# Keys' squares read from the diagonal of their products with one another, in a gated-delta-rule kernel

## The chip, the cores and the metric

The kernel runs on one core of one Trainium2 chip. The metric is the device time of one launch in microseconds, the median of several runs. The engines are called by the names of the profile: PE (TensorE; PEld is its weight load), DVE (VectorE), ACT (ScalarE), POOL (GpSimd) and SP (SyncE, which only issues transfers here).

## The reference

Four sequences of 512 tokens and 512 channels pass through two blocks. The first mixes channels over time (`cond`), projects to queries, keys, values and gates, runs a gated delta rule over chunks in 16 query/key heads and 32 value heads of 128, and projects back; the second mixes again (`cond2`) and applies a binarized linear layer. What the change touches is the norm of the keys and what uses it:

```python
k = _rmsnorm(k) * inv                       # x * rsqrt(mean(x*x, -1) + eps), per token and head
k_beta = k * beta[..., None]
M = where(stril, einsum('bhncd,bhnmd->bhncm', k_beta, k) * decay, 0)
T = solve_triangular(eye + M, eye, lower=True)
v_c = T @ v_beta;  k_cumdecay = T @ (k_beta * exp(g))
...                                         # scan over the chunks with a state of 128 x 128
```

The kernel uses chunks of 128 tokens. It never scales the keys themselves: the reciprocal root `rk` of each token's sum of squares is folded into factors for each token and value head (`br`, `nbr`, `nbe`).

## The kernel before

The work is cut into 64 units, one for each sequence (batch) and query/key head, `n = 16 * batch + head`. One loop step `i` interleaves pieces of five units: `K` (six ahead: the keys of unit i+6 are made and their matrix prepared), `F` (the front of unit i: values, queries, the inverse), `C` (the chunk recurrence of the unit before), `O` and `W` (its output, two and three before). The interleaving is written out by hand in `plan` (L937), a list of 22 slots; each engine executes its own instructions in exactly the order in which the slots issue them. Nothing is reordered by a scheduler.

What is issued in which slot, as far as it matters here (slots counted from 0):

- slots 5 to 7: `project(K, 1)` makes the keys' projection on PE; `tap` and `taps` (L486) apply the 4-tap convolution, the first tap on ACT into a tile `y`, three more on DVE, each adding to `y` from the PSUM tile `ps_p`.
- slot 8: `silu(K, 1)` (L490) on ACT gives the keys `k`, features on partitions. Slot 9: `square(K, 1)` (L496) on ACT.
- slot 11: `norms(K, 1)` (L501) on PE, four products of a square's 128x128 block with a column of ones, so that each token's sum of squares stands on its own partition (`pss`). In the trace each product is two weight loads and two products, eight rows in all.
- slot 12: `key_norm(K)` (L555) on DVE adds the epsilon, and `root_start` (L512) makes a first guess of the reciprocal root with two integer instructions; `key_root(K)` (L562) refines it on POOL and makes the factors `br`, `nbr`, `nbe`. After `key_norm`, in the same slot, DVE has the last scan of the channel mixing, where there is one.
- slot 13: `taps(F, 3)` on DVE. Slot 14: the state update of chunk 2 (`chunk_t_end`, L856) on DVE, silu of slab 3 on ACT.
- slot 16: `chunk_r(C, 3)` and `key_pairs(K)` (L578) on PE: each chunk's keys times themselves, into a PSUM bank `ps_kk`; also the tap of slab 0 and `chunk_r_end` (L804, the tile `r`) on DVE.
- slots 17 and 18: `key_matrix(K)` (L585) on DVE multiplies `ps_kk` by `nbr` and the decay; `chunk_w(C, 3)` (L821) on PE uses `r`.
- slots 19 and 20: `key_blocks` (L597) and `inverse_load` (L648) issue transfers on SP.

Some units also carry a channel-mixing job (`"wkv"` entries; `EXTRA`, L1015): heads 3, 4, 5 and 7 mix the first block's input for the next batch, heads 9, 11, 12 and 13 the second block's. Such a job puts four scans, a long reciprocal and, at slot 18, `wkv_end` (L307) on DVE; for the second block it also stores its result through SP. In batch 0 the units transpose the raw weights, too, which adds work on PE and ACT; later batches load them transposed. Head 8 of the first three batches computes the gates of the next batch.

PSUM banks come in four tags, with 2, 3, 1 and 2 buffers (`banks`, L90). `ps_kk` shares the single `inv` bank with the steps of the triangular inverse (slots 3 to 11) and with the query products (slot 20).

Before the loop the keys of the first six units are made in a start-up of their own (`first_norm`, L1140): their norms are collected in one tile, one root is taken for all, and then `key_pairs` and `key_matrix` follow for each.

## Time and profile before

| what | value |
|---|---|
| median of 3 runs | 3418.11 us (3409.30 to 3420.46) |
| the profiled execution: time, span | 3405.61 us, 3403.5 us |
| mean granted TensorE clock | 0.972 |
| PE busy | 3235.8 us, 95% |
| DVE busy | 2125.1 us, 62% |
| ACT busy | 1854.7 us, 54% |
| POOL busy | 1453.4 us, 43% |
| DMA, mean | 96 GB/s |

The spans of the units follow from the starts of `chunk_w` of chunk 0 on PE: about 46.1 us without channel mixing in batches 1 to 3, 46.9 with the second block's and 48.2 with the first block's, and some 3.5 us more in batch 0. A busy share is an average over all of these. In a timeline each row gives the start, the time from the first to the last instruction of a merged group, the engine, the source line (here always that of the recording helper, so one goes by the tiles), the operation, the tiles as out<-in, the shapes, how many instructions are merged, and in brackets the engine's idle time before it with what ended it. A row for PE that ends after the next one starts is normal: products are pipelined.

### The profile page before, as it was taken

What the parts mean: (1) busy time and instruction counts of PE and PEld (TensorE: products, weight loads), DVE (VectorE), ACT (ScalarE), POOL (GpSimd) and SP (SyncE); (2) the same over time, 40 slices, a digit from 0 to 9 for tenths busy, and PEclk for the clock granted to TensorE, in tenths of its full rate; (3) what the DMA queues carried; (4) which work ended last, traced back from release to release, by engine and by line L of the source; (5) the groups of instructions that cost most, each with busy time, mean ns of one, the idle gap of its engine ahead of it and who ended that gap; (6) DMA issues with size and microseconds to landing.
All of it is one profiled execution on the core that took longest, in us unless ns stands there. A gap on an engine that the chain in (4) does not pass through costs nothing.

```text
span 3403.5 us, 57390 instructions
## 1 busy us (share of the span) xinstructions
PE 3235.8 (95%) x20096; PEld 2232.8 (66%) x20096; DVE 2125.1 (62%) x4443; ACT 1854.7 (54%) x5016; POOL 1453.4 (43%) x3018
## 2 busy tenths in 40 slices
PE   6659999999999999999999999999999999999968
PEld 3336767767767666677766667667777667766634
DVE  7345766667656777667665777767755656667420
ACT  2436666666665655555555655555565556555411
POOL 3315445264533647265533556264624334453011
PEclk8669999999999999999999999999999999999978
DMA  2224434344434323234223332234332233232132
GB/s 69 91 63 113 139 116 125 113 121 139 125 105 134 99 67 96 81 93 120 73 86 103 108 87 87 62 95 119 87 96 80 92 90 99 80 90 71 44 101 78
DMA packets 424704, 326.51 MB, mean 96 GB/s; under 512 B 217377, under 2 KB 332577, under 8 KB 423394
## 3 DMA queue, kind: packets, MB, share of 16 engines
q1 hardware_dynamic: 420194, 320.75, 32.0%
q8 instruction: 161, 2.64, 0.3%
q10 hardware_dynamic: 4224, 2.10, 0.2%
q14 instruction: 125, 1.02, 0.1%
HBM read 251.18 MB, written 71.57 MB: 95 GB/s over the span
## 4 chain that ended last, share of the span: by engine, by line
PE 79%; DVE 8%; ACT 4%; issue 3%; DMA 2%; SPq 0%; POOL 0%; ACTq 0%; POOLq 0%; DVEq 0%
PE ps_p L79 21%; PE ps_out L79 13%; PE ps_z L79 12%; PE ps_w L79 4%; PE ps_s L79 4%; PE ps_j L79 4%; PE ps_i L79 3%; PE ps_o L79 3%; DVE y L79 3%; PE pss L79 3%; PE ps_st L79 2%; PE ps_kq L79 2%; DVE f L79 2%; PE ps_h L79 1%; PE ps_v L79 1%
## 5 line engine op out<-in xcount | busy, mean ns | idle before, releaser
L79 PE MATMUL ps_p<-cT,w 128*128 128x512 f32 x2000 | 948.9, 606 | 13.5 <-ACT w L79 13.5
L79 DVE SCALAR_TENSOR_TENSOR y<-ps_p,cw,y 128x511 f32<-128x511 f32 (+2 forms) x768 | 570.6, 743 | 474.5 <-ACT y L79 460.9
L79 PEld LDWEIGHTS ps_p<-cT,w 128*128 128x128 f32 x2000 | 349.2, 191 | 329.9 <-issue 274.6
L79 PE MATMUL ps_z<-w,cT 128*128 128x256 f32 x2048 | 476.5, 379 | 0.0
L79 PE MATMUL ps_out<-hT,wo 128*128 128x512 f32 x1024 | 463.7, 596 | 0.0
L79 PEld LDWEIGHTS ps_z<-w,cT 128*128 128x128 f32 x2048 | 373.7, 190 | 42.5
L79 PEld LDWEIGHTS ps_out<-hT,wo 128*128 128x128 f32 x1024 | 184.7, 190 | 186.2 <-issue 168.3
L79 DVE TENSOR_TENSOR xT<-xT,ps_out 128x512 f32<-128x512 f32 x256 | 174.8, 683 | 183.7 <-PE ps_out L79 183.3
L79 POOL TENSOR_TENSOR L<-L,t 128x30 f32<-128x30 f32 (+14 forms) x450 | 262.6, 584 | 35.3
L79 POOL TENSOR_TENSOR rs_t_k<-rs_y_k 128x4 f32<-128x4 f32 x174 | 48.3, 277 | 522.5 <-DVE rs_y_k L79 513.4
L79 ACT ACTIVATE qs<-ps_s,eg 128x128 f32<-128x128 f32 x384 | 120.1, 363 | 261.1 <-DVE r L79 259.7
L79 POOL TENSOR_TENSOR dkd<-dkd,far_d 128x1024 f32<-128x1024 f32 x64 | 151.3, 2365 | 255.2 <-DMA dkd<-gsc 210.2
L79 DVE SCALAR_TENSOR_TENSOR o<-o,rs_y_o,nz 128x128 f32<-128x128 f32 x512 | 238.2, 521 | 3.7 <-POOL rs_y_o L79 3.7
L79 POOL TENSOR_TENSOR t<-L 128x30 f32<-128x30 f32 (+14 forms) x450 | 224.7, 499 | 30.3
L79 ACT ACTIVATE dkt<-dkt,gsum 128x128 f32<-128x128 f32 x512 | 162.9, 392 | 130.2 <-POOL dkt L79 130.1
L79 ACT ACTIVATE y<-ps_p,cw 128x512 f32<-128x512 f32 x256 | 175.2, 684 | 75.9 <-PE ps_p L79 65.6
L79 ACT ACTIVATE wd<-ps_w,eg 128x128 f32<-128x128 f32 x384 | 119.6, 364 | 164.5 <-PE ps_w L79 163.1
L79 ACT ACTIVATE junk<-o 128x128 f32<-128x128 f32 x512 | 157.7, 308 | 90.3 <-DVE o L79 82.3
L79 ACT ACT_TABLE_LOAD x131 | 168.1, 1283 | 71.0 <-DVE y L79 55.0
L79 POOL TENSOR_TENSOR rs_t_o<-rs_y_o 128x8 f32<-128x8 f32 x192 | 38.6, 201 | 372.0 <-DVE rs_y_o L79 361.9
L79 POOL TENSOR_TENSOR dkt<-dkt,far_t 128x1024 f32<-128x1024 f32 x64 | 152.3, 2379 | 84.9 <-DMA dkt<-gsc 64.3
L79 ACT ACTIVATE v<-y 128x512 f32<-128x512 f32 x128 | 80.7, 630 | 176.0 <-DVE y L79 175.4
(269 smaller groups left out, 6096.1 us busy)
## 6 DMA issues: line engine op xcount, KB each, us to landing
w<-wsc SPq DMA_DIRECT2D x288, 256.0 KB, 5.4
dkd<-gsc SPq DMA_DIRECT2D x64, 512.0 KB, 4.6
dkt<-gsc SPq DMA_DIRECT2D x64, 512.0 KB, 4.4
wraw<-in_L_attn_W_qkvz_dram SPq DMA_DIRECT2D x96, 256.0 KB, 3.0
wo<-wosc SPq DMA_DIRECT2D x96, 256.0 KB, 3.5
wsc<-w SPq DMA_DIRECT2D x90, 256.0 KB, 2.1
blocks_m<-dkd SPq DMA_DIRECT2D x256, 32.0 KB, 1.7
L<-blocks_m SPq DMA_DIRECT2D x16, 512.0 KB, 5.3
```

The costliest lines, as they stand in the source:

```text
L79: return lambda *args, **kw: tc.keep_in_program_order(op(*args, **kw))
```

## The change

The keys' sums of squares are no longer made by ACT and PE. `key_squares` on DVE multiplies `ps_kk`, the keys' products with one another, by the identity, four blocks of 128 at once, and sums each row: what remains is the diagonal, each token's sum of squares. For this the pairs are made four slots sooner, behind `project(F, 3, 1)`, and `key_norm` and `key_root` move one slot later, ahead of the taps of slab 3 in DVE's queue. `square(K, 1)` and `norms(K, 1)` leave the plan. At the start `first_norm` makes the pairs and reads their diagonal; the loop behind it, which is not in the diff, makes the pairs of these six units again.

```diff
+        def key_squares(n, out):
+            sq = u2p.tile([P, NC, P], F32, tag="y", name=f"sq_{n}")
+            V.tensor_tensor(sq, units[n]["kk"], bc(ident, 1, NC), ALU.mult)
+            V.tensor_reduce(out, sq, AX.X, ALU.add)
+            V.tensor_scalar_add(out, out, HD * EPS)
...
         def key_norm(n):
...
-            V.tensor_scalar_add(kn, u["pss1"], HD * EPS)
+            key_squares(n, kn)
...
-             (square, K, 1), (chunk_squares, C, 1), ("sub", 8, 28)],
+             (chunk_squares, C, 1), ("sub", 8, 28)],
...
-            [(project, F, 3, 0), (norms, K, 1), (slab_turn, F, 0), (inverse_4_end, F), (silu, F, 2),
+            [(project, F, 3, 0), (slab_turn, F, 0), (inverse_4_end, F), (silu, F, 2),
...
-            [(chunk_w, C, 2), (project, F, 3, 1), (chunk_w_end, C, 2), (key_norm, K), (key_root, K),
+            [(chunk_w, C, 2), (project, F, 3, 1), (key_pairs, K), (chunk_w_end, C, 2),
              (slab_end, F, 0), ("wkv", wkv_scan, "n", True), ("sub", 11, None)],
-            [(project, F, 0, 0), (turn, F, 2), (tap, F, 3, 0), (taps, F, 3), ...
+            [(project, F, 0, 0), (turn, F, 2), (key_norm, K), (key_root, K), (tap, F, 3, 0), (taps, F, 3), ...
...
-            [(chunk_r, C, 3), (key_pairs, K), (tap, F, 0, 0), (slab_end, C, 5), (turn_end, F, 1),
+            [(chunk_r, C, 3), (tap, F, 0, 0), (slab_end, C, 5), (turn_end, F, 1),
...
         def first_norm(n):
             silu(n, 1)
-            square(n, 1)
-            norms(n, 1)
-            V.tensor_scalar_add(kn[:, n * NC : (n + 1) * NC], units[n]["pss1"], HD * EPS)
+            key_pairs(n)
+            key_squares(n, kn[:, n * NC : (n + 1) * NC])
```

More of the change, by code (lines that the diff above doesn't have):

```diff
@@ L974 @@
              ("wkv", wkv_sum, "d"), (slab_start, C, 4), (slab_start, C, 5), ("sub", 9, 29)],
-            [(project, F, 3, 0), (norms, K, 1), (slab_turn, F, 0), (inverse_4_end, F), (silu, F, 2),
+            [(project, F, 3, 0), (slab_turn, F, 0), (inverse_4_end, F), (silu, F, 2),
              ("wkv", wkv_scan, "n", False), ("sub", 10, 30)],
-            [(chunk_w, C, 2), (project, F, 3, 1), (chunk_w_end, C, 2), (key_norm, K), (key_root, K),
+            [(chunk_w, C, 2), (project, F, 3, 1), (key_pairs, K), (chunk_w_end, C, 2),
              (slab_end, F, 0), ("wkv", wkv_scan, "n", True), ("sub", 11, None)],
-            [(project, F, 0, 0), (turn, F, 2), (tap, F, 3, 0), (taps, F, 3), ("store",), ("wkv", wkv_sum, "n"), (out_start, O, 0), ("sub", 12, None)],
+            [(project, F, 0, 0), (turn, F, 2), (key_norm, K), (key_root, K), (tap, F, 3, 0), (taps, F, 3), ("store",), ("wkv", wkv_sum, "n"), (out_start, O, 0), ("sub", 12, None)],
             [(chunk_t, C, 2), (slab_turn, C, 4), (chunk_t_end, C, 2), (silu, F, 3),
```

## The prediction

> **What bounds the kernel now.** The busy table comes first, then the stretches of single units of the main loop: a unit with no channel-mixing work (2026.0 to 2072.1 us) and one with it (1929.5 to 1977.7).

> ```profile
> PE 3235.8 (95%) x20096; PEld 2232.8 (66%) x20096; DVE 2125.1 (62%) x4443; ACT 1854.7 (54%) x5016; POOL 1453.4 (43%) x3018
> ...
> 2026.00:2072.10 46.10, 46.10 (x296) 32.07 (x295) 28.55 (x62) 26.03 (x73) 29.36 (x69) 1.00 0.34 95
> 1929.50:1977.70 48.20, 47.26 (x303) 32.94 (x302) 36.75 (x73) 28.22 (x78) 20.47 (x37) 1.00 0.30 85
> ```

> PE fills the plain unit without a gap; in the other 0.94 us are open, so there something else is already late. Next, PE and DVE in order of time in the plain unit:

> ```profile
> 2052.05 0.95 PE L79 MATMUL pss<-ones,sq 128*128 128x1 f32 x8
> 2052.86 0.69 PE L79 MATMUL ps_w<-r,inv_t 128*128 128x128 f32 x4
> 2053.39 3.60 PE L79 MATMUL ps_p<-cT,w 128*128 128x512 f32 x8
> ...
> 2064.22 0.61 PE L79 MATMUL ps_w<-r,inv_t 128*128 128x128 f32 x4
> ...
> 2056.03 2.32 DVE L79 SCALAR_TENSOR_TENSOR y<-ps_p,cw,y 128x511 f32<-128x511 f32 x3 [2.42 <-ACT y L79]
> ...
> 2062.12 0.60 DVE L79 SCALAR_TENSOR_TENSOR r<-ps_s,nbe,vb 128x128 f32<-128x128 f32 x2
> ```

> The key norm holds PE 0.81 us from its start to the next start, and the row behind it keeps 0.53 us to its successor where later ones keep 0.44. The first half of `r` ends at about 2062.46; PE asks for it at 2064.22 (`chunk_w` of chunk 3): 1.7 us of slack. The unit with channel mixing:

> ```profile
> 1960.12 1.22 DVE L79 TENSOR_TENSOR_SCAN b<-decay,ekv 128x512 f32<-128x512 f32 x1
> 1961.25 2.29 DVE L79 SCALAR_TENSOR_TENSOR y<-ps_p,cw,y 128x511 f32<-128x511 f32 x3
> ...
> 1965.49 3.35 DVE L79 RECIPROCAL f<-f 128x512 f32<-128x512 f32 x1
> 1968.76 0.65 DVE L79 SCALAR_TENSOR_TENSOR y<-ps_p,cw,y 128x511 f32<-128x511 f32 x1
> 1969.33 0.60 DVE L79 SCALAR_TENSOR_TENSOR r<-ps_s,nbe,vb 128x128 f32<-128x128 f32 x2
> ...
> 1969.72 0.75 PE L79 MATMUL ps_w<-r,inv_t 128*128 128x128 f32 x4 [0.57 <-DVE r L79]
> ```

> Here DVE has no pause from the scans to `r`, and PE already waits for `r` at this very place. What enters DVE's queue ahead of `r` lengthens such a unit by its full time. So I read the kernel as PE-bound in plain units and DVE-bound, in this stretch, in the others.

> [...] the `xT` row has 683 with one operand in PSUM. [...] the only reduce here (`tf<-tcond`, 512 to 4) took 686 ns. [...]

> **The change, part by part.** Unit counts: 57 units (1 to 57) make keys in steady state. With the batch-0 units apart: 25 later ones without channel mixing, 8 later ones mixing the first input, 9 the second; in batch 0 seven, four and four. The sum is against the profiled execution, 3405.6 us (span 3403.5); the median of the runs is 3418.1, 12.5 higher, and I add the difference to that.

> *Removed on PE.* The program's order shows 256 fewer key-norm products and 24 more key pairs (first six units, which remake them in the loop). Per unit 0.81 us plus 0.07 to 0.09 behind it: 0.88 later, 0.85 in batch 0 (extra weight transposes; 0.48 behind it). All of it exposed would be 42 x 0.88 + 15 x 0.85 = 50 us.

> *Removed on ACT.* One 0.63 us square per unit, 0.53 of the queue. It brings DVE's first tap of slab 2 forward by 0.39 in mixing units (the 0.32 us pause for ACT `y` there, and the overlap of instructions that follow at once), and in batch 0 cuts a 0.73 us PE wait for ACT `w` to 0.20. Elsewhere ACT has pauses: nothing.

> *Added on DVE.* A product of 128x512 from PSUM (0.68), a reduce (0.69), an addition (0.16), each 0.03 to 0.04 after the one before: 1.63 us, then the two root instructions as before; 1.92 from the first start to the next tap. The old small addition and roots took 0.44. Bounds for the 1.63: 1.2 if both passes overlap like independent ones (`ps_kq` rows: 0.61 apart), 2.1 if each stretches to 0.9. I take 1.63.

> *Moved.* The key pairs (0.90 us on PE) go from behind `chunk_r` 3 to behind the `ps_p` of slab 3: PE time unchanged up to there. Their bank is free: `inv_t` is copied out at 2052.7, they start at 2054.2. The norm moves from ahead of a scan to ahead of the three taps of slab 3, and now waits for the pairs. Queued behind it on DVE: taps, state, `o`, tap of slab 0, `r`, key matrix. ACT waits for the taps (silu), then DVE again for ACT's `y`. POOL's root starts some 3.5 us later in plain units and ends at about 2061.8; the key matrix needs it at 2065.4. The group-inverse step moved ahead of the root fills the time that it waits. The later masks delay `out_scale` some 1.5 us, against 2 to 3 us of slack in the head transposes: nothing, or up to 1 us in 14 units if that cover is short.

> *Plain units, later batches.* The pairs end 1.05 + 0.03 after their start. To the taps 1.92, to their end 2.32, then ACT's unbroken silu-to-`y` stretch and DVE's tap and half of `r`, 4.11 (2058.35 to 2062.46): `r` stands 9.47 us after the pairs' start (0.04 to reach PE). PE's own work between is 9.10. Wait 0.37; net -0.88 + 0.37 = -0.51, x25 = -12.8. State is ready at 2060.06 against 2060.32: no wait. Batch 0 has a further transpose or two on PE: no wait, 7 x -0.85 = -6.0.

> *First-input units.* DVE-bound: +1.92 - 0.44 - 0.39 = +1.08 at `r`, and the unit grows by that: x8 = +8.6. In batch 0 there was about 0.6 slack and 0.53 comes back at ACT `w`: +0.15 x4 = +0.6.

> *Second-input units.* `r` 1.26 later, 0.5 of slack before: about +0.76 x9 = +6.9; batch 0: -0.05 x4 = -0.2.

> *SP.* In second-input units its queue waits for `wkv_end`, which stands behind all this on DVE, and only then issues a store, three loads or stores and the next unit's inverse loads.

> ```profile
> 1599.77 0.32 SPq L79 DMA_DIRECT2D base<-ek  x1
> 1600.18 0.38 SPq L79 DMA_DIRECT2D dkd<-gsc  x1
> 1600.62 0.45 SPq L79 DMA_DIRECT2D w<-wsc  x1
> 1601.16 1.87 SPq L79 DMA_DIRECT2D blocks_m<-dkd  x4
> 1603.13 0.40 SPq L79 DMA_DIRECT2D inv_t<-blocks_t  x1
> ```

> The last of those loads is issued at 1606.75 and takes some 1.8 us; PE starts `ps_i` at 1608.52 and its second half 0.46 later: almost no slack. Relative to PE SP comes 0.5 us later (1.3 in batch 0): about 0.1 to 0.4 us each for nine units and 0.4 to 1.2 for four, +5 together (0 to 9). In plain units SP comes 1.7 later, with 2.4 to 4 us spare in all but a few: nothing.

> *Start.* Before the loop each norm ran on PE, now pairs and norm share the one `inv` bank and DVE also makes the taps: the last norm is ready some 2.1 us later. In unit 0 the taps come 0.7 later, and DVE's own inverse follows them. Together +2.8 (1 to 5).

> Sum: -12.8 - 6.0 + 8.6 + 0.6 + 6.9 - 0.2 + 5 + 2.8 = **+5 us**: 3410 for such an execution, 3423 against the median. 0.3% is 10 us, about what a measurement of this kernel tells from no change.

> **Rivals.** *No change, as summed* (0.47; 3423): the saved weight loads reappear as waits for `r`. Speaking for it: PE waits for `r` there already.

> *Faster* (0.20): DVE's additions are shorter or overlap, so plain units keep all 0.88 (-9), mixing units lose half (-8) and SP lands in time (-5): 3401. The far end, nothing of DVE's work on the path, would be about 3371; the waits for `r` in the trace speak against it.

> *Slower* (0.33): the DVE step is longer, from PSUM, by 0.3 us. 42 later units carry each tenth, 4.2 us, and batch 0 and SP about 1 more: +18, 3441; typically 3433. It decides from 0.1 us on, since +5 then becomes +10. For it: I have only one reduce to price by. [...]

> *It does not do what it says*: excluded by the program's order, which has 256 norm products for queries alone.

> **How the numbers follow.** Predicted 3423. The range runs from the faster case's value, less 2 us for a cheaper start, 3399, to the slower case's end, 3441; what lies beyond both, 3371 among it, is given the remaining 2 in 10. Chances: faster by over 0.3% 0.20, within 0.47, slower 0.33.

> **What would show it.** Right: PE's instruction count falls by 464; waits of PE `ps_w` for DVE `r` (now 14 times, 10.6 us in the list of waits) come in most units, about 0.4 us in plain and 1.5 to 2.5 in mixing ones; plain units near 45.6, first-input ones near 49.3, second-input ones near 47.7. Wrong: units of 45.2 with no gap (DVE was hidden), or a wait ahead of the taps longer than the three instructions, or PE waiting for the pairs' bank.

## The result, and the profile after

The changed kernel took 3454.95 us in the median of four runs (3451.50 to 3456.56), the kernel before 3416.03 (3409.30 to 3420.46). The ratio is 1.0114, with a 95% interval of 1.0095 to 1.0134: **slower by 39 us**, where +5 was predicted. The profiled execution after took 3456.56 us with a span of 3454.4; against the one of before the span grew by 50.9 us. Of that, 12 us are not in the medians and so no effect of the change: the profiled execution of before was 10.4 us shorter than its median, the one of after 1.6 longer.

The first line of the page's busy table, after:

```profile
PE 3222.3 (93%) x19632; PEld 2194.6 (64%) x19632; DVE 2199.2 (64%) x4571; ACT 1811.0 (52%) x4952; POOL 1443.1 (42%) x3018
```

PE has 464 rows less and is 13.5 us less busy; DVE has 128 instructions more. The work went where it was meant to go, and PE now waits for longer than it saved. Next, the table of windows for three single units of the changed kernel: a plain one of a later batch, one that mixes the first input, and a plain one of batch 0. Columns: window, its length, then each engine's busy time with its instructions, the granted clock of PE, the DMA share and GB/s.

```profile
2067.92:2113.68 45.76, 45.53 (x288) 31.26 (x287) 28.41 (x64) 25.42 (x72) 26.95 (x65) 1.00 0.31 92
1965.98:2016.90 50.92, 48.30 (x295) 33.40 (x295) 38.36 (x75) 27.65 (x77) 19.69 (x37) 0.97 0.30 82
903.20:954.10 50.90, 49.34 (x316) 34.06 (x315) 27.76 (x65) 29.10 (x79) 31.89 (x71) 1.00 0.44 128
```

The same units took 46.12, 48.25 and 49.65 us before. The plain one gained 0.36, the mixing one lost 2.7 with a clock below 1.00, and the batch-0 one lost 1.2, where a gain of 0.85 was predicted. From the list of PE's waits after (what waited, for what: us in total, times, longest):

```profile
PE ps_w L79 <- DVE r L79: 43.3, 47, 2.3
...
PE ps_i L79 <- DMA inv_t<-blocks_t: 15.7, 8, 10.1
...
PE ps_z L79 <- ACT w L79: 11.8, 16, 0.7
...
PE ps_w L79 <- ACT vb L79: 7.8, 16, 0.5
...
PE ps_j L79 <- DVE nw L79: 6.3, 11, 0.8
```

The same list of before has 10.6 us in 14 waits for `r`, 11.2 in 3 at `ps_i`, 3.7 in 9 at `ps_j`, and neither the third line nor the fourth. The wait for `r` had been predicted, and it comes in every unit from 17 to 57; the two on ACT, 19.6 us in units 1 to 16, had not.

Summing the lengths of the units (from the start of `chunk_w` of chunk 0 to the next one on PE; units are numbered by the loop step) gives where the span grew, in us. The 5 us put down for SP stand whole in the row of the later second-input units, though some 3 of them were meant for batch 0.

| part | predicted | profile |
|---|---|---|
| up to unit 1 | +2.8 | +6.0 |
| units 1 and 2 | -1.7 | +4.2 |
| batch 0, units 3 to 15 | -3.9 | +9.7 |
| 25 later plain units | -12.8 | -4.1 |
| 8 later first-input units | +8.6 | +20.1 |
| 9 later second-input units, with SP | +11.9 | +12.3 |
| units 58 to 64 | 0 | -0.4 |
| the last stage, after the loop | 0 | +3.0 |

Of the first row, 3.7 us were lost before the first instruction that the change touches (`ps_g` starts at 86.70 us, before at 83.05), and 1.7 more by the time the pairs of the second prepared unit are made again (131.01 against 125.62). Units 1 and 2 include a half-clock stretch of PE that lasts 64.9 us where it lasted 54.6. The last stage is not touched by the change. Nor does the first row say much of it: in the profiles of the experiments below it lies between 0.0 and 4.3 us above before in five kernels with the start of before, and between 3.8 below and 4.8 above in five with the changed start.

**A plain unit**, in order of time, DVE and then PE:

```profile
2097.24 0.69 DVE L79 TENSOR_TENSOR sq<-ps_kk,ident 128x512 f32<-128x512 f32 x1 [2.89 <-PE ps_kk L79]
2097.97 0.69 DVE L79 TENSOR_REDUCE kn<-sq 128x4 f32<-128x512 f32 x1
2098.69 0.17 DVE L79 TENSOR_SCALAR kn<-kn 128x4 f32<-128x4 f32 x1
...
2099.18 2.31 DVE L79 SCALAR_TENSOR_TENSOR y<-ps_p,cw,y 128x511 f32<-128x511 f32 x3
...
2096.15 1.05 PE L79 MATMUL ps_kk<-k 128*128 128x128 f32 x8
...
2105.66 0.75 PE L79 MATMUL ps_w<-r,inv_t 128*128 128x128 f32 x4 [0.23 <-DVE r L79]
2106.24 3.62 PE L79 MATMUL ps_z<-w,cT 128*128 128x256 f32 x16
```

From the product's start to the taps 1.94 us (predicted 1.92), from the pairs' start to `chunk_w` of chunk 3 9.51 (predicted 9.47). PE comes 0.39 us late (predicted 0.37), of which the bracket shows 0.23. What the working left out is the row after it: `ps_z` starts 0.58 us behind `ps_w`, where a PE that has not waited keeps 0.44. (The weight load of the row's first product starts together with it, at 2105.66; without a wait, as in the unit of before at 2064.22, it starts 0.11 us ahead.) So -0.88 + 0.39 + 0.14 = -0.35, where -0.51 had been worked out.

**A first-input unit** has the same row with a wait of 2.25 us, and behind it a slow PE: 16 `ps_z` products take 4.85 us instead of the 3.62 above. The trace's clock records have a stretch of 3.4 us at half clock from 2007.4.

```profile
2007.30 1.20 PE L79 MATMUL ps_w<-r,inv_t 128*128 128x128 f32 x4 [2.25 <-DVE r L79]
2008.29 4.85 PE L79 MATMUL ps_z<-w,cT 128*128 128x256 f32 x16
```

**A batch-0 unit**. First before, ACT and then PE:

```profile
919.58 0.63 ACT L79 ACTIVATE v<-y 128x512 f32<-128x512 f32 x1 [2.46 <-DVE y L79]
...
921.87 0.60 PE L79 MATMUL ps_w<-ident,wraw 128*128 128x128 f32 x4
...
924.06 1.89 PE L79 MATMUL ps_z<-w,cT 128*128 128x256 f32 x8
```

Neither product waits. After, PE and then ACT:

```profile
940.78 0.66 PE L79 MATMUL ps_w<-ident,wraw 128*128 128x128 f32 x4 [0.48 <-ACT vb L79]
...
943.04 1.99 PE L79 MATMUL ps_z<-w,cT 128*128 128x256 f32 x8 [0.74 <-ACT w L79]
...
939.06 0.63 ACT L79 ACTIVATE v<-y 128x512 f32<-128x512 f32 x1 [4.50 <-DVE y L79]
939.60 1.13 ACT L79 ACTIVATE vb<-ps_v,br 128x128 f32<-128x128 f32 x4
940.60 0.60 ACT L79 COPY w<-ps_w 128x512 f32<-128x512 f32 x1
...
942.41 0.57 ACT L79 COPY w<-ps_w 128x512 f32<-128x512 f32 x1
```

ACT stands 4.50 us at the silu of slab 3 instead of 2.46; the silu waits for DVE's taps, now behind the key squares. Behind it in ACT's queue stand the four `vb`, which free the bank that PE's next weight transposes take, and the weight copies that the `ps_z` products read. PE waits for the first, then for the second.

### The profile page after: what moved, and what is told of

Read it like the earlier page. It is cut to its first block, busy times and chain, and to the rows that moved or that the text cites. A ratio compares the mean times of both kernels' runs of the same rounds, so it can differ in the third digit from the quotient of the medians.

```text
span 3454.4 us, 56475 instructions
## 1 busy us (share of the span) xinstructions
PE 3222.3 (93%) x19632; PEld 2194.6 (64%) x19632; DVE 2199.2 (64%) x4571; ACT 1811.0 (52%) x4952; POOL 1443.1 (42%) x3018
## 3 DMA queue, kind: packets, MB, share of 16 engines
q14 instruction: 126, 1.03, 0.1%
## 4 chain that ended last, share of the span: by engine, by line
PE 59%; DVE 19%; ACT 6%; issue 4%; POOL 4%; DMA 3%; SPq 1%; ACTq 0%; POOLq 0%; DVEq 0%
PE ps_p L79 15%; PE ps_out L79 11%; PE ps_z L79 9%; DVE y L79 6%; PE ps_j L79 4%; PE ps_w L79 4%; PE ps_i L79 3%; DVE f L79 3%; PE ps_s L79 3%; PE ps_o L79 2%; DVE o L79 2%; DVE kn L79 1%; PE ps_kq L79 1%; PE ps_st L79 1%; PE ps_h L79 1%
## 5 line engine op out<-in xcount | busy, mean ns | idle before, releaser
L79 PE MATMUL ps_p<-cT,w 128*128 128x512 f32 x2000 | 960.2, 607 | 10.7 <-ACT w L79 10.4
L79 DVE SCALAR_TENSOR_TENSOR y<-ps_p,cw,y 128x511 f32<-128x511 f32 (+2 forms) x768 | 569.3, 741 | 357.7 <-ACT y L79 343.8
L79 PEld LDWEIGHTS ps_p<-cT,w 128*128 128x128 f32 x2000 | 346.9, 191 | 298.8 <-issue 264.9
L79 PE MATMUL ps_z<-w,cT 128*128 128x256 f32 x2048 | 485.6, 384 | 11.8 <-ACT w L79 11.8
L79 PE MATMUL ps_out<-hT,wo 128*128 128x512 f32 x1024 | 465.2, 597 | 0.0
L79 PEld LDWEIGHTS ps_z<-w,cT 128*128 128x128 f32 x2048 | 382.4, 193 | 65.1 <-ACT w L79 18.2
L79 POOL TENSOR_TENSOR rs_t_k<-rs_y_k 128x4 f32<-128x4 f32 x174 | 34.9, 201 | 655.7 <-DVE rs_y_k L79 646.6
L79 PEld LDWEIGHTS ps_out<-hT,wo 128*128 128x128 f32 x1024 | 185.3, 191 | 187.1 <-issue 169.9
L79 DVE TENSOR_TENSOR xT<-xT,ps_out 128x512 f32<-128x512 f32 x256 | 174.7, 683 | 199.2 <-PE ps_out L79 199.0
L79 POOL TENSOR_TENSOR t<-L 128x30 f32<-128x30 f32 (+14 forms) x450 | 250.2, 556 | 30.3
L79 DVE SCALAR_TENSOR_TENSOR o<-o,rs_y_o,nz 128x128 f32<-128x128 f32 x512 | 245.7, 535 | 23.2 <-POOL rs_y_o L79 23.2
L79 POOL TENSOR_TENSOR L<-L,t 128x30 f32<-128x30 f32 (+14 forms) x450 | 242.6, 539 | 35.3
L79 ACT ACTIVATE qs<-ps_s,eg 128x128 f32<-128x128 f32 x384 | 120.0, 363 | 254.9 <-DVE r L79 250.3
L79 ACT ACTIVATE dkt<-dkt,gsum 128x128 f32<-128x128 f32 x512 | 162.9, 392 | 154.5 <-POOL dkt L79 154.5
L79 POOL TENSOR_TENSOR dkd<-dkd,far_d 128x1024 f32<-128x1024 f32 x64 | 151.3, 2366 | 214.4 <-DMA dkd<-gsc 181.6
L79 ACT ACTIVATE v<-y 128x512 f32<-128x512 f32 x128 | 80.7, 630 | 283.4 <-DVE y L79 278.9
L79 ACT ACTIVATE y<-ps_p,cw 128x512 f32<-128x512 f32 x256 | 175.5, 686 | 82.7 <-PE ps_p L79 68.2
L79 POOL TENSOR_TENSOR dkt<-dkt,far_t 128x1024 f32<-128x1024 f32 x64 | 152.3, 2380 | 97.6 <-DMA dkt<-gsc 76.9
L79 ACT ACTIVATE junk<-o 128x128 f32<-128x128 f32 x512 | 157.7, 308 | 62.2 <-DVE o L79 54.1
L79 ACT ACTIVATE wd<-ps_w,eg 128x128 f32<-128x128 f32 x384 | 119.2, 363 | 121.8 <-PE ps_w L79 118.6
L79 ACT ACTIVATE dkd<-dkd,gsum 128x128 f32<-128x128 f32 x512 | 156.7, 388 | 45.7 <-POOL dkd L79 45.2
```

Source lines behind the costliest of these rows:

```text
L79: return lambda *args, **kw: tc.keep_in_program_order(op(*args, **kw))
```

## The experiments

The kernel before ran beside each group again; its medians there were 3412 to 3415 us. **D** is the theory that the time goes into DVE's product and reduce ahead of the taps, and what stands behind those. Lengths of units are against the kernel before.

### The move without the squares

The kernel before with three entries of the plan moved:

```diff
-[(chunk_w, C, 2), (project, F, 3, 1), (chunk_w_end, C, 2), (key_norm, K), (key_root, K),
+[(chunk_w, C, 2), (project, F, 3, 1), (key_pairs, K), (chunk_w_end, C, 2),
-... (turn, F, 2), (tap, F, 3, 0), (taps, F, 3),
+... (turn, F, 2), (key_norm, K), (key_root, K), (tap, F, 3, 0), (taps, F, 3),
-[(chunk_r, C, 3), (key_pairs, K), (tap, F, 0, 0),
+[(chunk_r, C, 3), (tap, F, 0, 0),
```

> The kernel before with the moves alone: the key pairs behind the projection of slab 3, key_norm and key_root ahead of the taps of slab 3; ACT's square and PE's norm products stay. Theory D (what costs is DVE's 1.5 us of product and reduce ahead of the taps, and all that stands behind them on DVE and, through silu, on ACT): DVE's work is as before and the small addition waits for nothing, so within 4 us of before; batch-0 units keep their gaps as before (0.23 us, 0.97 with the first input). Rival M (the move itself costs: the pairs ahead of the rest of PE's queue, the later roots on POOL, later masks and loads): at least 15 us slower than before, with PE gaps at ps_z for ACT w or at ps_i for the inverse's loads.

Measured: 3425.84 us, ratio 1.003 (1.002 to 1.004), 11 us slower. Nearly all plain later units are unchanged to 0.01 us and batch 0 has no wait for weights at `ps_z`, so the move is not what cost 39. But it isn't free, and D had put it within 4 us: later mixing units grew by 0.1 (first input) and 0.25 us (second), and batch 0 by some 5 us in five of its units (in two of them PE waits 0.84 us for `r`). What delays it there was not followed up, so the cause of these 11 us is open.

### The squares without product and reduce

```diff
-            V.tensor_tensor(sq, units[n]["kk"], bc(ident, 1, NC), ALU.mult)
-            V.tensor_reduce(out, sq, AX.X, ALU.add)
-            V.tensor_scalar_add(out, out, HD * EPS)
+            V.tensor_scalar(out, units[n]["kk"][:, :, 0], HD * EPS, 1.0, ALU.add, ALU.max)
```

> The changed kernel without the product with the identity and without the reduce: the addition reads one column of each pairs block from PSUM instead (so the keys' roots are made from other numbers). The wait for the pairs and all moves stay; only some 1.45 us of DVE work per unit is gone. Theory D: later plain units lose 0.88 us against before (45.2), batch-0 units 0.85, second-input units about 0.88, first-input units about 0.4 (ACT's square no longer delays DVE); together about 45 us less than before, 85 less than the changed kernel. Rival M (the move and the wait for the pairs cost, not DVE's time): at most 20 us less than the changed kernel, still slower than before, and the batch-0 gaps at ps_z for ACT w stay.

Measured: 3372.79 us, ratio 0.9867 (0.9848 to 0.9885): 42 us faster than before, 81 less than the changed kernel. Plain later units -0.89 with no wait for `r`; first-input units -0.42; second-input units -0.53 in six of nine (the other three wait for inverse loads); batch 0 -0.3 to -1.3. The moves and the wait for the pairs are still there, the loss is not. This settles it for D: 1.45 us of DVE time in each of 57 units decides between -42 and +39.

### The norm behind the state update

The changed kernel with both entries one slot later:

```diff
-... (turn, F, 2), (key_norm, K), (key_root, K), (tap, F, 3, 0), (taps, F, 3),
+... (turn, F, 2), (tap, F, 3, 0), (taps, F, 3),
-             (turn_end, F, 2), ("soon", load_slice, "k"),
+             (turn_end, F, 2), (key_norm, K), (key_root, K), ("soon", load_slice, "k"),
```

> The changed kernel with key_norm and key_root put one slot later still, behind the state update and o of chunk 2 and ahead of the tap of slab 0, where DVE waits 2.75 us for ACT's y in plain units. Theory D: the taps of slab 3 and so ACT's weight copies are no longer delayed, batch-0 units lose their 1.22 us of gaps and end 0.85 below before (15 units, -13); plain units have no wait for r and end 0.8 to 0.88 below before (25, -20 to -22); units with channel mixing stay as in the changed kernel (+20 and +12); start +2: about equal to before to 5 us faster. Rival M (the later roots on POOL and the later key matrix reach SP and the inverse loads): PE gaps at ps_i of 0.5 us or more in most plain units, and slower than before by 10 us or more.

Measured: 3471.77 us, ratio 1.0162 (1.0145 to 1.0178), 57 us slower: neither theory. What D said of plain units holds (-0.89 in 17 of the 25 later ones, and no batch-0 wait for weights), but the eight first-input units lost 38 us together and the nine second-input ones 24, more than in the changed kernel. Something behind the norm got worse; the mixtures below show what.

### The start of before, the loop changed

```diff
         def first_norm(n):
             silu(n, 1)
-            key_pairs(n)
-            key_squares(n, kn[:, n * NC : (n + 1) * NC])
+            square(n, 1)
+            norms(n, 1)
+            V.tensor_scalar_add(kn[:, n * NC : (n + 1) * NC], units[n]["pss1"], HD * EPS)
```

> The changed kernel with the start of the kernel before (ACT squares and PE norms for the six first units), the loop as changed. Theory: the start costs 1 to 3 us, so 36 to 38 us slower than before. Rival S (the start costs the 6 us by which the first unit of the loop began later in the profile, and 3 more in unit 1): 30 us or less slower than before.

Measured: 3449.62 us, ratio 1.0098 (1.0080 to 1.0116), 35 us slower. The intervals of this ratio and of the changed kernel's overlap: the start costs a few us at most, and not more can be said.

### ACT's order

```diff
-            [(chunk_t, C, 2), (slab_turn, C, 4), (chunk_t_end, C, 2), (silu, F, 3),
-             (turn_end, F, 2), ("soon", load_slice, "k"), ...
+            [(chunk_t, C, 2), (slab_turn, C, 4), (chunk_t_end, C, 2), (turn_end, F, 2), (slab_end, C, 4), (silu, F, 3),
+             ("soon", load_slice, "k"), ...
-... (slab_turn, C, 5), (slab_end, C, 4),
+... (slab_turn, C, 5),
```

> The changed kernel with ACT's order altered in slot 14: turn_end of slab 2 (the four vb) and slab_end of slab 4 (a weight copy, batch 0 only) go ahead of the silu of slab 3. Theory A (batch 0 lost because these two stand in ACT's queue behind the silu that now waits longer for DVE's taps): the two PE gaps of batch-0 units, 0.48 at ps_w for ACT vb and 0.74 at ps_z for ACT w, go; those units fall from 0.85 us above before to 0.3 to 0.85 below it, which is 12 to 25 us over batch 0 and the first unit behind it: 14 to 27 us slower than before instead of 39. Later batches stay as in the changed kernel. Rival B (PE itself asks too early for a bank or a weight, whatever ACT's order): batch-0 units keep about 1.2 us of gaps, the time stays within 5 us of the changed kernel's.

Measured: 3437.31 us, ratio 1.0072 (1.0058 to 1.0085), 25 us slower than before, 14 less than the changed kernel. The wait at `ps_w` for `vb` is gone from PE's list, and the one for the weights has shrunk:

```profile
PE ps_z L79 <- ACT w L79: 2.8, 16, 0.2
```

Units 3 to 15 cost 2.8 us in place of 9.7. Theory A is right on batch 0. I had not expected the rest: most later plain units fell to -0.89 as well, which is the larger part of the gain. In those too the `vb` (1.13 us) stood on ACT between the silu and the `y` that DVE's next tap waits for; ahead of the silu they fill ACT's wait, and the wait for `r` is gone. First-input units cost 24.7 us, 6 of 8 with half-clock stretches. The order was not altered in the kernel before, where PE is busy throughout a plain unit (46.10 of 46.10 us) and has no such wait to lose.

### Without the reduce

```diff
-            V.tensor_reduce(out, sq, AX.X, ALU.add)
-            V.tensor_scalar_add(out, out, HD * EPS)
+            V.tensor_scalar(out, sq[:, :, 0], HD * EPS, 1.0, ALU.add, ALU.max)
```

> The changed kernel without DVE's reduce: the addition takes one column of each block of the product instead (so the keys' roots are made from other numbers); 0.72 us less on DVE per unit. Theory D with a threshold for each kind of unit: later plain units lose their 0.5 us at r altogether (45.2 us, 0.88 below before), first-input units end 0.3 above before, second-input units 0.2 above, batch-0 units 0.0 to 0.2 above; 8 to 14 us faster than before. On the clock: PE's wait for r in first-input units falls from 2.25 to about 1.5 us. Theory H (a wait of over 2 us there makes the clock fall to one half for 3.4 us, worth 1.7 us): no half-clock stretch in any first-input unit. Rival C (half-clock stretches come at random): four or five in these units again.

Measured: 3399.49 us, ratio 0.9962 (0.9948 to 0.9975), 13 us faster. Plain later units -0.89, first-input units +0.31 (+0.91 to +0.99 in units 19, 23, 35 and 39), second-input ones +0.20 in five of nine and up to +0.70 in the others, plain and second-input batch-0 units mostly +0.1 to +0.3. With half of the added DVE time the change would have paid: the price is not linear, there is a threshold in each kind of unit. PE's wait for `r` in first-input units is 1.77 us, and the clock records have no half-clock stretch between 300 and 3250 us.

### The mixture

Steps with channel mixing keep the old norm, the others take the new one, behind the state update; the start is that of before:

```diff
+            if mixing(n):
+                V.tensor_scalar_add(kn, u["pss1"], HD * EPS)
+            else:
+                key_squares(n, kn)
...
-             (square, K, 1), (chunk_squares, C, 1), ("sub", 8, 28)],
+             ("mix", square, K, 1), (chunk_squares, C, 1), ("sub", 8, 28)],
...
+             (turn_end, F, 2), ("plain", key_norm, K), ("plain", key_root, K), ("soon", load_slice, "k"),
```

> A mixture: steps without channel mixing take the new norm, with key_norm and key_root behind the state update and o of chunk 2 (where plain units of the late-norm kernel ended 0.90 us below before); steps with channel mixing take the old norm (ACT's square, PE's norm products, pairs and key_norm in their old places), and so does the start. Theory D: 25 later plain units at -0.90, seven batch-0 units at -0.65 to -0.85, the others unchanged: 25 to 29 us faster than before. Rival M (SP and the inverse loads come late through the later key matrix): 10 us or less of it is left, with PE gaps at ps_i in plain units.

Measured: 3430.31 us, ratio 1.0059 (1.0045 to 1.0073), 18 us slower; the expectation was missed by 45 us. Most plain units have their -0.89, most mixing units their old length. But mixing units 3, 7, 19, 23, 27, 35 and 43 are 1.3 to 3.4 us longer, unit 39 9.4 (with 10.2 us at half clock), and the later plain ones among those with numbers 3 modulo 4 (31, 47, 51, 55) 1.3 to 3.0. Unit 28, behind 27, waits 1.6 us for its inverse loads. In units with numbers 2 and 3 modulo 4 POOL makes the group inverse, one step (`t`, `L`) with each slot, and the root stands in the same queue. Theory G of the following runs is that the root, waiting for DVE's `key_norm`, holds back the group steps behind it.

### The root moved on POOL

In the mixture, and as a second kernel in the changed one, `key_root` alone is put at the end of slot 16:

```diff
-             (turn_end, F, 2), ("plain", key_norm, K), ("plain", key_root, K), ("soon", load_slice, "k"),
+             (turn_end, F, 2), ("plain", key_norm, K), ("soon", load_slice, "k"),
-             (chunk_q_end, C, 3), ("sub", 15, None)],
+             (chunk_q_end, C, 3), ("sub", 15, None), ("plain", key_root, K)],
```

> The mixture with key_root of the plain steps moved likewise, behind the group steps of slots 12 to 16. Theory G: the units with numbers 3 modulo 4, which were 1.3 to 3.4 us longer than before (one 9.4) in the mixture, and those that followed with late inverse loads, return to before's lengths (channel mixing) or to 0.9 below (plain); plain units stay at -0.90: 24 to 29 us faster than before. Rival L (what was late is the key matrix behind the later norm, not POOL's group steps): those units stay long and it is not faster than before by more than 5 us.

Measured: 3388.60 us, ratio 0.9927 (0.9908 to 0.9946): 25.5 us faster than before, 44 less than the mixture, each against its own runs of before. The mixing units that had grown are within 0.02 us of before, the plain ones mostly at -0.89; of the later units only 28 (+3.7), 44 (+1.0) and 46 (+2.0) stand out, which wait 0.7 to 1.7 us for inverse loads at `ps_i`; why the loads come late there was not tested. POOL's timeline in unit 22 of the mixture, which starts at 1272.6, and of this kernel, where it starts at 1265.9:

```profile
1307.46 0.20 POOL L79 TENSOR_TENSOR rs_t_k<-rs_y_k 128x4 f32<-128x4 f32 x1 [13.56 <-DVE rs_y_k L79]
...
1323.07 2.35 POOL L79 TENSOR_TENSOR dkd<-dkd,far_d 128x1024 f32<-128x1024 f32 x1
```

```profile
1300.80 0.20 POOL L79 TENSOR_TENSOR rs_t_k<-rs_y_k 128x4 f32<-128x4 f32 x1 [9.28 <-DVE rs_y_k L79]
...
1312.13 2.35 POOL L79 TENSOR_TENSOR dkd<-dkd,far_d 128x1024 f32<-128x1024 f32 x1
```

In the mixture POOL stands 13.56 us at the root with the rest of the group steps behind it, and the next unit's mask starts 50.5 us after the unit's start; with three steps let past the root it starts at 46.2. Theory G is shown.

In the changed kernel, the root moved in every step:

> The changed kernel with only key_root moved on POOL: from slot 13 to the end of slot 16, behind the steps of the group inverse that slots 12 to 16 issue. Theory G (in units whose number is 2 or 3 modulo 4 POOL also makes the group inverse; the root that waits longer for DVE's key_norm holds those steps back, and the mask, out_scale and nw of the next unit come late): in first-input units 19, 23, 35 and 39 the wait at ps_j for nw falls from 0.85 us to 0.37 and they end about 0.8 us lower, PE's other waits stay; some 3 to 6 us less than the changed kernel, still 33 us or more slower than before. Rival N (POOL's order does not matter there): those units stay at 1.8 us or more above before.

Measured: 3494.23 us, ratio 1.0238 (1.0217 to 1.0259), the slowest of all. The wait at `ps_j` did fall to 0.37 us in the four units. But in mixing units the root now stands behind the channel mixing's three POOL products, and a wait of 1.5 to 2.0 us at `ps_s` for `state` came in the later ones, one of 1.5 to 2.5 us at `ps_w` for `vb` in those of batch 0. DVE and POOL in unit 20 show it:

```profile
1248.61 1.25 DVE L79 TENSOR_SCALAR kn<-kn 128x4 f32<-128x4 f32 x1
...
1250.10 1.12 DVE L79 TENSOR_SCALAR rs_y_k<-rs_t_k 128x4 int32<-128x4 int32 x1
...
1248.57 1.26 POOL L79 TENSOR_TENSOR d<-d,k 128x512 f32<-128x512 f32 x1
1249.91 1.27 POOL L79 TENSOR_TENSOR ek<-ek,d 128x512 f32<-128x512 f32 x1
```

Two DVE instructions that took 0.17 us take 1.25 and 1.12 and end as POOL's products end (1249.86 against 1249.83, 1251.22 against 1251.18); the 2.03 us that they lose are the wait of 2.02 us at `ps_s` in this unit. With the root ahead, POOL's products had waited until DVE was past them: in this unit of the changed kernel DVE's last one starts at 1230.16 and POOL's first product at 1235.36.

### The root moved in plain steps alone

The same edit in the changed kernel, with `("mix", key_root, K)` kept behind `key_norm`.

> The changed kernel with key_root moved behind the group steps of slots 12 to 16 in steps without channel mixing only; in mixing steps it stays ahead of the channel mixing's POOL sums. Theory G: units 19, 23, 35 and 39 fall by about 0.8 us with the wait at ps_j back at 0.37, units 27 and 43 by 0.3 to 0.6, and the 2 us at ps_s for state, which came when key_root was moved in all steps, are absent: 3 to 10 us less than the changed kernel (half-clock stretches can add), 29 to 36 us slower than before. Rival N (key_root so late costs by itself, through the key matrix): plain units grow and it is slower than the changed kernel.

Measured: 3447.39 us, ratio 1.0096 (1.0077 to 1.0115), 34 us slower than before. All eight first-input units have 0.37 us at `ps_j` and 2.25 at `ps_w`, and no wait at `ps_s`. So only the clock tells them apart: five take 50.9 to 51.0 us, three 49.3. The table of windows of two of them, units 35 and 39:

```profile
1903.50:1954.46 50.96, 48.34 (x295) 33.35 (x295) 39.31 (x75) 29.71 (x78) 31.11 (x58) 0.97 0.36 104
2102.20:2151.47 49.27, 46.65 (x296) 32.11 (x295) 39.25 (x75) 29.61 (x78) 31.02 (x58) 1.00 0.33 98
```

The three at full clock are 1.03 us longer than before; the prediction had 1.08. A half-clock stretch of 3.4 us adds 1.7.

### The old norm in first-input units

The changed kernel, with the old norm and its old places in steps that mix the first input.

```diff
+            if first_input(n):
+                V.tensor_scalar_add(kn, u["pss1"], HD * EPS)
+            else:
+                key_squares(n, kn)
...
```

> The changed kernel, but steps that mix the first input (units 3, 4, 5 and 7 of each batch but the last) keep the old norm with ACT's square, PE's norm products and everything in its old place. Theory: the eight later ones of these units, which cost 20 us in the changed kernel (8.2 for DVE's time at r, 3.3 for POOL's late group, 8.4 for five half-clock stretches), cost at most the 3.3 of POOL: 15 to 19 us less than the changed kernel, 20 to 24 slower than before; PE's wait for r there is 0.56 us and no half-clock stretch lies in them. Rival C (half-clock stretches are chance): 8 to 12 us less only, with three or more stretches in these units.

Measured: 3438.82 us, ratio 1.0064 (1.0048 to 1.0081), 26 us slower: 13 less than the changed kernel, where 15 to 19 were expected. The eight units cost 3.26 us, 0.8 in each of 19, 23, 35 and 39 and nothing in the others, which is POOL's part as expected, and none has a half-clock stretch. In the profiled execution late inverse loads cost more elsewhere (units 14 and 29: +6.3 and +6.5, with 6.8 us at half clock in each); whether this is why the median fell by less is not shown.

### The early norm in the mixture

The mixture with the root moved, but `key_norm` of plain steps ahead of the taps as in the change, and ACT's order as above.

> The same, with key_norm of the plain steps where the change has it, ahead of the taps of slab 3, and ACT's order in slot 14 altered (the four vb and the copy of slab 4 ahead of the silu of slab 3). Theory D with A: plain later units again 0.90 below before, batch-0 plain units about 0.4 below; 22 to 27 us faster than before, and some 2 us slower than or equal to the late norm, unless the later key matrix costs there (rival L), in which case this one is the faster by 10 us or more.

Measured: 3392.49 us, ratio 0.9937 (0.9919 to 0.9955). Within the intervals it equals the late norm: once neither POOL's nor ACT's queue is held up, the place on DVE makes no difference that was measured. Both are faster than the kernel before and the changed one.

## Why the prediction was wrong

**Right.** PE's bound in plain units, DVE's in mixing ones. The price of the DVE step: 1.94 us against 1.92. The wait for `r` as the place where the saving comes back, and its size: 9.51 us from the pairs to `chunk_w` against 9.47. First-input units +1.03 (predicted +1.08; the terms add up to 1.09) where the clock held; second-input units +0.92 where nothing but `r` is waited for (+0.76, without the restart). Late inverse loads: PE's waits at `ps_i` come to 2.7 us in second-input units 28, 29 and 45 and to 4.0 in units 30 and 42 behind such units, 1.7 of it half clock; 5 (0 to 9) had been put down. That SP was late through `wkv_end` was not tested: the mixture with the root moved has such waits, too, with the old norm in its mixing steps.

**Right by luck.** In batch 0 first-input units grew by 0.19 to 0.20 us in three of four, and +0.15 had been worked out, but from `r`: PE waits for `r` in none of them, and for `vb` and weights in all. The slower rival had the side and not the reason: the DVE step was not longer. (Its +18 us is some 2 too many by its own terms, three tenths at 4.2 and 1 us each; the result lies beyond it either way.)

**Wrong, by the steps of the sum.**

- *Batch 0, "a further transpose or two on PE: no wait".* The step looked at `r` only. The taps of slab 3 are also what ACT's silu waits for, 4.50 us in the unit shown, and the `vb` (939.60) and the weight copies (940.60, 942.41) come behind the silu (939.06) in ACT's rows: they came late, and two PE waits of 0.48 and 0.74 came in every such unit; with the slow rows behind them they cost 1.7 us. Plain ones mostly ended at +0.85 in place of -0.85; units 3 to 15 cost 9.7 us in place of -3.9. The prediction named ACT's silu as waiting, and did not list what is queued behind it. Shown by ACT's order altered.
- *First-input units, the clock.* The term had no clock in it. Behind a wait of 2.25 us PE fell to half clock in five of eight units, five times 1.69 us, 8.4 in all. Shown by the two lengths, 50.96 and 49.27 us, and by the kernels without the reduce and with the old norm in these units, in which the wait is 1.77 and 0.56 us and no such stretch lies in them. Which five it is, is told by where the wait falls (last section).
- *POOL, "nothing, or up to 1 us in 14 units" for the later masks.* Of the group inverse only the step moved ahead of the root was looked at, not the steps behind it. They cost 0.8 us in each of four first-input units and 0.6 in units 27 and 43, 4.5 together, which are gone where the root moves in plain steps; with the norm later still it is what made the mixture slow.
- *Plain units, the wait for `r`.* 0.14 us of slow restart behind each wait was left out; with the 0.02 by which the wait was longer, units end 0.15 above the sum, 25 x 0.15 = 3.7 us.

These parts are read from the two profiles, so they are to be set against the profiles' difference: 50.9 us where 4.9 had been summed, a miss of 46 (34 against the medians). Batch 0 with 13.6 us, the clock with 8.4, POOL with 4.5 and the restart with 3.7 make 30 of them. Units 1, 2 and 16, which have the same two waits on ACT, add 7. The start and the last stage add 6, of which most may be the difference between two executions; the rest is small. What the start contributes is not resolved, nor why the move alone costs 11.

## What to carry to other kernels

When a step is moved or lengthened on an engine that runs its instructions as they were issued (in the mixture POOL stood 13.56 us at the root with the group steps behind it), list for every consumer of its result the instructions behind the consumer in *its* queue, and for them again: here the loss lay two queues away, in weight copies and group steps that have nothing to do with the keys' norm. Here a new wait cost more than its length: 0.14 us of restart in plain units, and 1.69 us at half clock in five of eight first-input units. Where the work fits depends on the unit, so choose the place per unit: the new norm only where DVE has a pause, and its root where POOL's other work isn't behind it, turned 1.1% slower into 0.7% faster.
